# Carry copies on ScalarE, ten instead of eight states shared with GpSimd, an earlier front of the second chunk, and square-root tables loaded ahead

## The chip, the core and the metric

The kernel runs on one core of one Trainium2 chip. A core has five engines with a queue of instructions each: PE (TensorE, matrix products), DVE (VectorE), ACT (ScalarE), POOL (GpSimd) and SP (SyncE, which here issues most DMA transfers). The metric is the device time of one launch in microseconds. Before the change the median of three runs is 9530.28 us (9522.71 to 9545.77).

## The reference: what is computed

Four images of 256 channels and 64 x 64 points go through four layers, each of the form x = x + layer(group_norm(x)), one after the other:

- layer 0: a deformable 3 x 3 convolution, whose sampling points come from a convolution of the input,
- layer 1: attention over all 4096 points,
- layer 2: a second deformable convolution with 16 groups,
- layer 3: a selective state-space layer (Mamba), which reads the image as a sequence of 4096 points.

Each normalization needs sums over the whole image, so a layer can't begin its main work before the last point of the one before is there. Each ends with a square root and a reciprocal.

The change is mostly about layer 3. Cut to what matters there (512 inner channels d, 16 states n):

```
u, res = split(in_proj(x));  u = silu(causal_conv4(u) + conv_b)
dt, B, C = split(x_proj(u));  delta = softplus(dt_proj(dt) + dt_b)
for each point l:
    state[d, n] = exp(delta[d] * A[d, n]) * state[d, n] + delta[d] * u[d] * B[n]
    y[d] = sum_n state[d, n] * C[n]
out = out_proj((y + u * D) * silu(res))
```

## The kernel before

The images are worked on one after the other. `layer0`, `layer1`, `layer2` and `layer3` each get the image in SBUF as 2 x 128 channels by 4096 points (`x`).

**Layer 3** cuts the sequence into NC = 8 chunks of C = 512 points. In the scan loop a step s is one chunk j = s // 16 and one state n = s % 16, so there are 128 steps per image. The inner channels are four groups of 128 partitions (`dc` 0 to 3). A step does this:

- `product(s)` (line 1480, DVE): h = du * B[n] for all four groups, where du = delta * u. In a *helped* step DVE makes only three groups, and POOL makes the fourth into `hq` (`quarter`, line 1472), with a B row that SP fetches two steps ahead (`ahead`, tile `bs`). DVE's own B row `bn` is a matmul result in PSUM (`state`, line 1465).
- `scan(dc)`, four times: ACT makes da = exp(delta * A) into PSUM (line 1560), and DVE scans h along the chunk (line 1562). The pool for `da` has two buffers, so that the exponential of scan i waits for scan i - 2.
- the last column of the four scans is copied to `carry` for the same state of the next chunk (line 1582, POOL),
- POOL multiplies the whole h by C[n] (line 1585), in place,
- PE adds the four groups of h into the chunk's `y` in PSUM (line 1443), two steps later.

While chunk j - 1 is scanned, the *front* of chunk j (`front(j)`) makes its inputs: projections, causal convolution, Silu, then delta by way of Exp, two Identity operations and Ln on ACT (lines 1362 to 1378), three additions and the multiplication that makes `du` on POOL (lines 1371 to 1382). ACT splits the B rows into two bf16 parts (`split`, lines 1347 to 1355), POOL subtracting the first part in between. `close(j)` ends a chunk: `gated` on DVE (line 1531) and the output projection.

The order is written out by hand: the loop runs in `manual_schedule` for PE, ACT, DVE and POOL, and every engine works through its queue in the order of the program. `put(step, half, pe, rest)` gives the place of each piece of a front. Front j begins at loop step 16 (j - 1) - 5, and at 16 (j - 1) - 2 for j = 1, whose first steps are done by `first()` ahead of the loop. Half 0 is after the second scan of a step, half 1 after the fourth and ahead of the carry copy, half 2 after the multiplication by C. The single PSUM bank of the front (`bank()`) is handed from one piece to the next.

At the steps in `visits`, `product(s + 1)` is put in the middle of step s, between its second and third scan. These are the steps in which ACT does Silu and changes its function tables twice: step 5 of chunk 0 and step 2 of chunks 1 to 7.

**The normalizations.** `stats` collects means and variances on DVE, averages them over groups by two small matmuls, and takes the root on ACT (line 175, `rs`), which needs the table set with Sqrt. `scaled` and layer 3's opening wait for `rs`.

Of the kernel before, what the change touches and what calls it, by code (L numbers as in the profile page):

```python
# [9 lines left out]
F32 = mybir.dt.float32  # L10
I32 = mybir.dt.int32
BF16 = mybir.dt.bfloat16
AF = mybir.ActivationFunctionType
# [3 lines left out]
P = 128  # L17
# [6 lines left out]
NCH = N // 512  # L24
# [4 lines left out]
DS = 16  # L29
# [34 lines left out]
class Net:  # L64
# [346 lines left out]
    def layer1(self, x):  # L411
# [4 lines left out]
        with tc.tile_pool(name="l1a", bufs=1) as pa, tc.tile_pool(name="l1b", bufs=2) as pb:  # L416
# [167 lines left out]
            def divide(qb):  # L584
                b = blocks[qb]
                pd = wide("pden")[:, 0, :4]
                for t in range(4):
                    for i in range(2):
                        nc.tensor.matmul(  # L589
                            pd[:, t : t + 1],  # L590
                            b["acc"][:, bass.ds(512 * i + P * t, P)],
                            self.ones[:, 0:1],
                            start=(i == 0),
                            stop=(i == 1),
                        )
                b["rc"] = pb.tile([P, 4], F32, tag="rc", name="rc")
                nc.vector.reciprocal(b["rc"], pd)

            def spread(qb):

# [69 lines left out]
    def layer2(self, x):  # L670
# [5 lines left out]
        with (  # L676
# [196 lines left out]
            with tc.manual_schedule(  # L873
                engines={
                    mybir.EngineType.PE,
                    mybir.EngineType.Activation,
                    mybir.EngineType.DVE,
                    mybir.EngineType.Pool,
                }
            ):  # L880
                values(0)
                for t in range(T):
                    offsets(0, t)
                hats(0, 0)
# [12 lines left out]
                hats(1, 0)  # L897
                hats(1, 1)


                behind = None
                for p in range(last + 1):
                    near, far = p < last, p < last - 1
                    for wy in range(WIN):
                        product(p, wy, 0)
                        if near and wy == 0:
                            masked(p + 1)
                        product(p, wy, 1)
                        if wy == 1 and p > 1:
                            finish(p - 2)  # L910
                        if near and wy > 1:
                            gather(p + 1, wy - 2)
                        if near and wy < 3:
                            outer(p + 1, wy, nc.gpsimd)
                        prod = pairs(p)
                        if behind:
                            total(*behind)
                        behind = p, wy, prod
                        if wy == 0:
                            if near:  # L920
                                clear(p + 1)
                            if p:
                                nc.scalar.copy(made[p - 1]["o"].rearrange("p t c -> p (t c)"), made[p - 1]["pd"])
                        if far and wy < 2:
                            offsets(p + 2, wy)
                        if wy == 2:
                            if far:
                                hats(p + 2, 0)
                            if p < last:
                                values(p + 3)  # L930
                        if wy == 3:
                            if far:
                                hats(p + 2, 1)
                            if p:
                                turned(p - 1)
                        if wy == 4 and p:
                            project(p - 1)
                total(*behind)
                nc.scalar.copy(made[last]["o"].rearrange("p t c -> p (t c)"), made[last]["pd"])
                finish(last - 1)  # L940
                turned(last)
                project(last)
                finish(last)
# [137 lines left out]
    def layer3(self, x, out, nxt, early):  # L1081
# [10 lines left out]
        with (  # L1092
# [166 lines left out]
            def front(j):  # L1259
# [15 lines left out]
                put(0, 0, None, begin)  # L1275

                for dc in range(4):
                    at = ((0, 1), (1, 0), (1, 1), (4, 1))[dc]
                    put(*at, *project(j, dc, lambda dc=dc: c["up"][:, dc, 3:]))

                def convolve(dc):
# [58 lines left out]
                def split(i):  # L1340
# [21 lines left out]
                put(11, 0, None, lambda: nc.scalar.activation(c["du"], c["du"], AF.Exp, scale=-1.0))  # L1362
# [5 lines left out]
                put(12, 0, None, one)  # L1368


                put(11, 2, None, lambda: nc.gpsimd.tensor_add(c["delta"], c["delta"], c["du"]))
                put(
                    13,
                    1,
                    None,
                    lambda: nc.scalar.activation(c["du"], c["w"], AF.Identity, bias=self.ones[:, 0:1], scale=-1.0),
                )
                put(14, 1, None, lambda: nc.scalar.activation(c["w"], c["w"], AF.Ln))
# [3 lines left out]
                put(last, 2, None, lambda: nc.gpsimd.tensor_mul(c["du"], c["delta"], c["u"]))  # L1382
# [150 lines left out]
            with tc.manual_schedule(  # L1533
# [14 lines left out]
                for s in range(total):  # L1548
# [30 lines left out]
                    scan(2)  # L1579
                    scan(3)  # L1580
                    empty(s, 1)
                    nc.gpsimd.tensor_copy(carry[:, :, n : n + 1], h[:, :, C - 1 : C])  # L1582
                    cn = c.pop(("cn", n))
                    if s + 1 < total:
                        nc.gpsimd.tensor_mul(h, h, cn.to_broadcast([P, 4, C]))  # L1585
# [143 lines left out]
```

## Time and profile before

| | us |
|---|---|
| median of three runs | 9530.28 |
| profiled execution | 9708.01 |
| its span | 9706.1 |
| last image: layer 0, from `rs` to `rs` (7291.4 to 7837.9) | 546.5 |
| last image: layer 1 (to 8345.9) | 508.0 |
| last image: layer 2 (to 8734.1) | 388.2 |
| last image: layer 3 (to the end) | 972.0 |

| engine | busy us in the span | share |
|---|---|---|
| PE | 8526.4 | 88% |
| DVE | 7498.5 | 77% |
| POOL | 7032.0 | 72% |
| ACT | 4909.6 | 51% |

The table of stages is read from the ACT instruction that makes `rs`, which marks the start of each layer. The shares of busy time are averages over layers with different limits. In a row of the profile, `x` is the number of instructions, `|` is followed by the busy time in us and the mean of one in ns, and behind the next `|` stands the idle time of that engine just before these instructions, with what ended it. In rows in order of time the first two numbers are the start and the length in us.

### The profile page before, as it was taken

The page shows a single profiled execution, that of the slowest core. Times are in us where ns is not written, and L with a number is a line of the kernel's source. Part 1 is how long each engine was busy: PE and PEld are TensorE (multiplying, and loading weights), DVE is VectorE, ACT ScalarE, POOL GpSimd, SP SyncE. Part 2 cuts the span into 40 slices and gives each one's busy share as a digit, 9 for nine tenths or more (in the row PEclk, how much of TensorE's full clock was granted, in tenths as well). Part 3 has the DMA queues.
Part 4 walks back from the last instruction along what each step waited for, and adds up shares of the span by engine and source line. Part 5 has one row for each costly group of instructions (what it writes and reads, how often), then busy time and mean ns, then how long its engine had stood idle before and what let it go on. Part 6 is the DMA issues. An engine that isn't in the chain of part 4 may idle for free. (4 is left out here: it accounts for less than half of the span.)

```text
span 9706.1 us, 89200 instructions
## 1 busy us (share of the span) xinstructions
PE 8526.4 (88%) x29097; PEld 4207.1 (43%) x29097; DVE 7498.5 (77%) x8203; ACT 4909.6 (51%) x7568; POOL 7032.0 (72%) x4164
## 2 busy tenths in 40 slices
PE   4789998998778999899878899989987789998997
PEld 3643353443464344344346434434435643443443
DVE  4864498999676459899968645989996764588998
ACT  3743335665474333566557433366655743326664
POOL 3746686998574668699857467879984746777997
PEclk9999999999899999999989999999998999999999
DMA  7940011222793001122279201112218820111121
GB/s 262 328 151 1 26 49 52 67 66 69 266 329 126 1 30 47 56 66 67 66 288 329 102 1 35 47 57 66 66 63 312 324 82 1 38 52 51 62 62 52
DMA packets 414120, 1022.66 MB, mean 105 GB/s; under 512 B 38644, under 2 KB 111789, under 8 KB 411597
## 3 DMA queue, kind: packets, MB, share of 16 engines
q0 software_dynamic: 165888, 604.05, 17.2%
q1 hardware_dynamic: 247756, 412.80, 13.4%
q8 instruction: 233, 3.82, 0.2%
q14 instruction: 243, 1.98, 0.1%
HBM read 849.60 MB, written 93.37 MB: 97 GB/s over the span
## 5 line engine op out<-in xcount | busy, mean ns | idle before, releaser
L1585 POOL TENSOR_TENSOR h<-h,cn 128x2048 f32<-128x2048 f32 x508 | 2301.0, 4530 | 41.3 <-POOL carry L1582 0.6
L1562 DVE TENSOR_TENSOR_SCAN h<-da,carry,h 128x512 f32<-128x512 f32 x1800 | 2172.5, 1264 | 83.7 <-ACT da L1560 35.3
L1560 ACT ACTIVATE da<-delta,l3a 128x512 f32<-128x512 f32 x2048 | 1398.0, 690 | 1300.0 <-DVE h L1562 1297.0
L1443 PE MATMUL y<-h,ident 128*128 128x512 f32 x4096 | 1931.5, 607 | 11.7 <-POOL h L1585 11.7
L344 POOL DMA_INDIRECT g<-tab,idx x1152 | 1359.4, 1180 | 744.3 <-issue 427.8
L565 POOL TENSOR_TENSOR acc<-acc,e 128x1024 f32<-128x1024 f32 x480 | 1126.0, 2346 | 540.3 <-ACT e L561 519.0
L388 PE MATMUL pz<-cols,l0w 128*128 128x256 f32 x4608 | 1213.2, 410 | 188.7 <-issue 84.5
L1443 PEld LDWEIGHTS y<-h,ident 128*128 128x128 f32 x4096 | 797.1, 195 | 1188.0 <-issue 1070.9
L353 DVE SCALAR_TENSOR_TENSOR r<-g,wx,r 128x512 f32<-128x512 f32 x1152 | 858.3, 745 | 376.6 <-ACT r L352 246.9
L462 DVE TENSOR_REDUCE m<-pm 128x3 f32<-128x1536 f32 (+2 forms) x340 | 599.5, 1763 | 700.2 <-PE pm L452 700.2
L388 PEld LDWEIGHTS pz<-cols,l0w 128*128 128x128 f32 x4608 | 894.9, 205 | 358.0 <-DVE cols L377 111.4
L1480 DVE TENSOR_TENSOR h<-du,bn 128x2048 f32<-128x2048 f32 (+1 forms) x512 | 1025.0, 2002 | 26.7 <-POOL du L1382 24.8
L561 ACT ACTIVATE e<-sc 128x1024 f32<-128x1024 f32 x512 | 496.1, 1020 | 1029.6 <-PE sc L548 1029.5
L572 PE MATMUL cx<-e,v 128*128 128x512 f32 x2048 | 1000.6, 616 | 0.0
L845 DVE TENSOR_TENSOR prod<-ring,A 128x1280 f32<-128x1280 f32 x640 | 922.5, 1480 | 69.9 <-DMA ring<-ring 54.9
L352 ACT ACTIVATE r<-g,wx 128x512 f32<-128x512 f32 x1152 | 826.2, 717 | 258.4 <-DMA g<-tab,idx 210.9
L862 PE MATMUL pacc<-prod,ident 128*128 128x512 f32 x1920 | 913.4, 611 | 26.5 <-DVE prod L845 17.9
L854 POOL TENSOR_TENSOR prod<-prod 128x512 f32<-128x512 f32 x640 | 800.9, 1276 | 176.6 <-DVE prod L845 154.0
L370 PE MATMUL pt<-ident,acc 128*128 128x128 f32 x2304 | 427.3, 292 | 285.7 <-DVE acc L361 202.2
L572 PEld LDWEIGHTS cx<-e,v 128*128 128x128 f32 x2048 | 352.5, 189 | 599.5 <-issue 596.9
L360 ACT ACTIVATE acc<-r,wy 128x256 f32<-128x256 f32 x1152 | 571.3, 496 | 14.9 <-DVE r L353 9.8
L361 DVE SCALAR_TENSOR_TENSOR acc<-r,wy,acc 128x256 f32<-128x256 f32 x1152 | 549.1, 477 | 0.3
(256 smaller groups left out, 11027.6 us busy)
## 6 DMA issues: line engine op xcount, KB each, us to landing
cn<-cd SPq DMA_DIRECT2D x512, 256.0 KB
tab<-vt SPq DMA_DIRECT2D x112, 640.0 KB
bs<-cd SPq DMA_DIRECT2D x248, 256.0 KB
ring<-ring SPq DMA_DIRECT2D x288, 126.0 KB
ring<-ring SPq DMA_DIRECT2D x288, 124.0 KB
g<-tab,idx POOLq DMA_INDIRECT x1152
x<-in_x SPq DMA_DIRECT2D x64, 256.0 KB
out<-x SPq DMA_DIRECT2D x56, 256.0 KB
```

Source lines behind the costliest of these rows:

```text
L344: nc.gpsimd.indirect_dma_start(out=g[:], out_offset=None, in_=tab[:, :], in_offset=bass.IndirectOffsetOnAxis(ap=idx[:, t, k : k + 1], axis=0),
L353: nc.vector.scalar_tensor_tensor(r, g[:, :, 1, :], wx[:, 1, t, k : k + 1], r, ALU.mult, ALU.add)
L388: nc.tensor.matmul(sums[m][:, ot, :256], wf[:, i, bass.ts(ot, P)], cols[m][:, i, :], start=(i == 0), stop=(i == 17),)
L565: nc.gpsimd.tensor_add(b["acc"], b["acc"], e)
L572: nc.tensor.matmul(blocks[qb]["cx"], v[:, 4 * (i + kt // 4 * 4) + kt % 4, :], e[:, bass.ts(i % 2, 512)], start=(kt == 0 and i == 0), stop= ...
L845: nc.vector.tensor_mul(d["prod"][:, :, t, :].rearrange("p x (g c) -> p x g c", c=GC), ring[y // VR % 4][:, :, y % VR, :].rearrange("p x (g ...
L862: nc.tensor.matmul(d["pd"], self.ident, prod[:, wx, :], start=(wy == 0 and wx == 4), stop=(wy == WIN - 1 and wx == 2),)
L1443: nc.tensor.matmul(c["ys", dc], self.ident, h[:, dc, :], start=False, stop=(n == DS - 1))
L1480: nc.vector.tensor_mul(h[:, :d, :], c["du"][:, :d, :], c.pop(("bn", n)).to_broadcast([P, d, C]))
L1560: nc.scalar.activation(da, c["delta"][:, dc, :], AF.Exp, scale=al[:, dc, n : n + 1])
L1562: nc.vector.tensor_tensor_scan(h[:, dc, :], da, hb, carry[:, dc, n : n + 1], ALU.mult, ALU.add)
L1585: nc.gpsimd.tensor_mul(h, h, cn.to_broadcast([P, 4, C]))
```

## The change

1. The copy of the scans' last columns to `carry` goes from POOL to ACT.
2. A step is helped if its state is not 6 to 11, and it is not one of the last four of chunk 0: ten states per chunk (0 to 5 and 12 to 15) in place of eight (0 to 5, 14, 15). Chunk 0 keeps six.
3. The front of chunk 1 has other places: the fourth projection is later, the first three pieces of the convolution half a step to a step later, and Exp, Identity, Ln, the splits, the gates and POOL's four operations one to two steps earlier.
4. For chunks 2 to 7 the multiplication that makes `du` moves from step 18 half 2 to step 19 half 1 of the front, which is from behind the multiplication by C of state 13 to ahead of that of state 14. The other places are the same.
5. The table set with Sqrt is loaded ahead: in layer 1 by a square root of the last block's reciprocal (its result is not used), at the ends of layers 2 and 3 by a preload.

```diff
@@ layer1, divide
                 nc.vector.reciprocal(b["rc"], pd)
+                if qb == NCH - 1:
+                    root = self.small.tile([P, 1], F32, tag="root", name="root")
+                    nc.scalar.activation(root, b["rc"][:, 0:1], AF.Sqrt)
@@ layer2, the end
                 total(*behind)
+                nc.scalar.preload_act_table_set("sqrt_and_others")
                 nc.scalar.copy(made[last]["o"].rearrange("p t c -> p (t c)"), made[last]["pd"])
@@ layer3, front
                 for dc in range(4):
-                    at = ((0, 1), (1, 0), (1, 1), (4, 1))[dc]
+                    at = ((0, 1), (1, 0), (1, 1), (4, 1) if j > 1 else (5, 0))[dc]
                     put(*at, *project(j, dc, lambda dc=dc: c["up"][:, dc, 3:]))
...
                 for dc in range(4):
-                    at = ((2, 1) if j > 1 else (3, 0), (3, 1), (5, 1), (6, 1))[dc]
+                    at = (((2, 1), (3, 1), (5, 1), (6, 1)) if j > 1 else ((3, 1), (4, 1), (5, 1), (6, 1)))[dc]
                     put(*at, *convolve(dc))
...
+                at = dict(e=(11, 0), w=(12, 0), c=(13, 1), ln=(14, 1), s=((11, 0), (12, 1), (15, 0)), sums=(11, 14, 16, 19))
+                if j == 1:
+                    at = dict(e=(10, 1), w=(11, 1), c=(12, 1), ln=(13, 0), s=((11, 0), (12, 0), (13, 1)), sums=(10, 12, 13, 15))
                 for i in range(3):
-                    put((11, 12, 15)[i], i == 1, None, split(i))
+                    put(*at["s"][i], None, split(i))
...
-                put(11, 2, None, lambda: nc.gpsimd.tensor_add(c["delta"], c["delta"], c["du"]))
...
-                last = 18 if j > 1 else 16
-                put(14, 2, None, lambda: nc.gpsimd.tensor_add(c["delta"], c["delta"], c["du"]))
-                put((14 + last) // 2, 2, None, lambda: nc.gpsimd.tensor_add(c["delta"], c["delta"], c["w"]))
-                put(last, 2, None, lambda: nc.gpsimd.tensor_mul(c["du"], c["delta"], c["u"]))
...
+                for step, part in zip(at["sums"], ("du", "du", "w")):
+                    put(step, 2, None, lambda part=part: nc.gpsimd.tensor_add(c["delta"], c["delta"], c[part]))
+                put(at["sums"][3], 1 if j > 1 else 2, None, lambda: nc.gpsimd.tensor_mul(c["du"], c["delta"], c["u"]))

                 for dc in range(4):
-                    at = ((14, 0), (14, 1), (15, 0), (15, 1)) if j > 1 else ((11, 1), (12, 0), (12, 1), (13, 1))
+                    at = ((14, 0), (14, 1), (15, 0), (15, 1)) if j > 1 else ((11, 0), (11, 1), (12, 0), (12, 1))
                     put(*at[dc], *gate(j, dc))
@@ layer3, the helped steps
-            hs, helped = {}, [s for s in range(NC * DS) if s % DS in (14, 15, 0, 1, 2, 3, 4, 5) and s // 2 != 7]
+            hs, helped = {}, [s for s in range(NC * DS) if s % DS not in range(6, 12) and s // 4 != 3]
@@ layer3, the loop
-                    nc.gpsimd.tensor_copy(carry[:, :, n : n + 1], h[:, :, C - 1 : C])
+                    nc.scalar.copy(carry[:, :, n : n + 1], h[:, :, C - 1 : C])
...
+                nc.scalar.preload_act_table_set("sqrt_and_others")
                 for a in late:
```

In the changed kernel's queues the fourth projection of chunk 1 stands behind the first half of the y additions of step 2, and a layer-2 copy of the first ring comes ahead of the table load for layer 3's Exp.

More of the change, by code (lines that the diff above doesn't have):

```diff
@@ L1357, in split @@
                     return part
+                at = dict(e=(11, 0), w=(12, 0), c=(13, 1), ln=(14, 1), s=((11, 0), (12, 1), (15, 0)), sums=(11, 14, 16, 19))
+                if j == 1:
+                    at = dict(e=(10, 1), w=(11, 1), c=(12, 1), ln=(13, 0), s=((11, 0), (12, 0), (13, 1)), sums=(10, 12, 13, 15))
                 for i in range(3):
-                    put((11, 12, 15)[i], i == 1, None, split(i))
-                put(11, 0, None, lambda: nc.scalar.activation(c["du"], c["du"], AF.Exp, scale=-1.0))
+                    put(*at["s"][i], None, split(i))
+                put(*at["e"], None, lambda: nc.scalar.activation(c["du"], c["du"], AF.Exp, scale=-1.0))
                 def one():
@@ L1366, in one, with over @@
                     nc.scalar.activation(c["w"], c["du"], AF.Identity, bias=self.ones[:, 0:1])
-                put(12, 0, None, one)
-                put(11, 2, None, lambda: nc.gpsimd.tensor_add(c["delta"], c["delta"], c["du"]))
[L1372 to L1378, printed above, removed]
-                last = 18 if j > 1 else 16
-                put(14, 2, None, lambda: nc.gpsimd.tensor_add(c["delta"], c["delta"], c["du"]))
-                put((14 + last) // 2, 2, None, lambda: nc.gpsimd.tensor_add(c["delta"], c["delta"], c["w"]))
-                put(last, 2, None, lambda: nc.gpsimd.tensor_mul(c["du"], c["delta"], c["u"]))
+                put(*at["w"], None, one)
+                def over():
+                    nc.scalar.activation(c["du"], c["w"], AF.Identity, bias=self.ones[:, 0:1], scale=-1.0)
+                put(*at["c"], None, over)
+                put(*at["ln"], None, lambda: nc.scalar.activation(c["w"], c["w"], AF.Ln))
+                for step, part in zip(at["sums"], ("du", "du", "w")):
+                    put(step, 2, None, lambda part=part: nc.gpsimd.tensor_add(c["delta"], c["delta"], c[part]))
+                put(at["sums"][3], 1 if j > 1 else 2, None, lambda: nc.gpsimd.tensor_mul(c["du"], c["delta"], c["u"]))
                 for dc in range(4):
-                    at = ((14, 0), (14, 1), (15, 0), (15, 1)) if j > 1 else ((11, 1), (12, 0), (12, 1), (13, 1))
+                    at = ((14, 0), (14, 1), (15, 0), (15, 1)) if j > 1 else ((11, 0), (11, 1), (12, 0), (12, 1))
                     put(*at[dc], *gate(j, dc))
```

## The prediction

> **What bounds the kernel now.** The profiled execution took 9708.01 us around a span of 9706.1; the median of the runs is 9530.28, so 178 us belong to profiling. I work out differences in microseconds on the trace and take them from the median. The change reaches layer 3's scan loop and the starts of the normalizations, so I read the loop first, by stretches: the first chunk of the last image and a middle one (columns: length, then busy time and count of PE, its weight loads, DVE, ACT, POOL; clock; DMA share; GB/s).
>
> ```profile
> 8769.27:8895.26 125.99, 111.82 (x257) 47.51 (x257) 109.19 (x82) 77.03 (x109) 98.60 (x44) 0.97 0.15 45
> 9006.44:9117.61 111.17, 106.29 (x253) 45.99 (x252) 109.71 (x85) 73.94 (x102) 105.39 (x49) 1.00 0.20 63
> ```
>
> A middle chunk is DVE from end to end: 109.71 of 111.17. POOL (105.4) and PE (106.3) have about 5 us of room. The first chunk has 15 us that no engine fills. Then the groups by shape, for the durations:
>
> ```profile
> L1562 DVE TENSOR_TENSOR_SCAN h<-da,carry,h 128x512 f32<-128x512 f32 x1800 | 2172.5, 1264 | 83.7 <-ACT da L1560 35.3 <-DVE h L1480 3.2 <-ACT sres L1245 0.5
> L1480 DVE TENSOR_TENSOR h<-du,bn 128x2048 f32<-128x2048 f32 x264 | 596.5, 2259 | 0.0
> L1480 DVE TENSOR_TENSOR h<-du,bn 128x1536 f32<-128x1536 f32 x248 | 428.5, 1728 | 26.7 <-POOL du L1382 24.8 <-PE bn L1465 1.3
> L1472 POOL TENSOR_TENSOR hq<-du,bs 128x512 f32<-128x512 f32 x248 | 316.4, 1276 | 21.1 <-issue 20.8
> L469 ACT CAST t<-mx 128x4 bf16<-128x4 f32 x96 | 18.6, 193 | 87.6 <-DVE mx L472 76.6 <-DVE mx L465 11.0
> ```
>
> A step is one product and four scans. In time order a full step repeats every 7.09 us, a helped one every 6.56. DVE's own order shows where the first chunk waits (the bracket is the idle time before):
>
> ```profile
> 8812.29 1.28 DVE L1562 TENSOR_TENSOR_SCAN h<-da,carry,h 128x512 f32<-128x512 f32 x1 [2.23 <-ACT da L1560]
> ...
> 8862.36 2.46 DVE L1562 TENSOR_TENSOR_SCAN h<-da,carry,h 128x512 f32<-128x512 f32 x2 [3.43 <-ACT da L1560]
> ...
> 8895.26 1.75 DVE L1480 TENSOR_TENSOR h<-du,bn 128x1536 f32<-128x1536 f32 x1 [5.85 <-POOL du L1382]
> ```
>
> With the smaller ones (0.66, 0.42, 1.75, 0.15, 0.81) that is 15.3 us per image. ACT at steps 1 and 2 of a middle chunk:
>
> ```profile
> 9019.67 0.69 ACT L1560 ACTIVATE da<-delta,l3a 128x512 f32<-128x512 f32 x1 [0.47 <-DVE h L1562]
> 9020.38 1.28 ACT L1301 ACT_TABLE_LOAD   x1
> ...
> 9026.70 1.30 ACT L1560 ACTIVATE da<-delta,l3a 128x512 f32<-128x512 f32 x2
> ```
>
> and POOL from step 9 to the `du` product of step 13:
>
> ```profile
> 8965.12 0.19 POOL L1582 COPY carry<-h 128x4 f32<-128x4 f32 x1 [1.05 <-DVE h L1562]
> 8965.40 4.54 POOL L1585 TENSOR_TENSOR h<-h,cn 128x2048 f32<-128x2048 f32 x1
> ...
> 8999.27 4.53 POOL L1382 TENSOR_TENSOR du<-delta,u 128x2048 f32<-128x2048 f32 x1
> ```
>
> E(n) below is the moment at which DVE may start what follows step n's last scan.
>
> **Ten helped states.** In steps 12 and 13 of chunks 1 to 7 POOL makes the fourth quarter of the product. DVE saves 7.09 - 6.56 = 0.53 us, 14 times per image, on the bound. POOL pays 1.22 us each (its repetition in the trace), and SP issues one more 256 KB broadcast two steps ahead of use. By the Trainium skill (GPSIMD Engine Reference, Key points) GpSimd shares its SBUF interfaces with VectorE and contends with DVE instructions that have two SBUF inputs, which speaks against this. The trace shows such a case: `du<-delta,u` in the opening takes 1.42 us beside a POOL subtraction and 0.69 without one. If every added quarter cost DVE that 0.73, it would eat the gain: 0.73 against 0.53. But the loop's products read `bn` and its scans `da` from PSUM, and scans beside POOL keep their 1.26 us. I take no contention: -7.4 us per image.
>
> **The carry copy on ACT.** DVE had no part in it; POOL loses 0.27 us per step. What it adds is a wait. ACT works in order, and `da` has two buffers, so until now ACT made the next step's first `da` once scan 2 was done, 1.2 us before E, and the second at E. Now both stand behind the copy, which waits for scan 3. The copy's cost is unseen on ACT; the nearest row is the 128x4 cast at 0.193. From E: copy at 0.12, first `da` at 0.30, ready at 1.0; the second starts at 0.94 instead of 0.11, so everything behind it is 0.82 later. Usually the next product (1.83 or 2.36 to the first scan) hides that. Three places lack the cover:
> - Visits: eight steps per image make the next product early, so scan follows scan (1.18 apart). There scan 0 now waits for the full 1.0 us.
> - Step 2: Silu and two table loads, 6.4 us, stand between `da` 1 and `da` 2. `da` 2 ended at 9027.36, scan 2 began at 9027.61: 0.22 of slack, so 0.6 us lost. Queued behind them, nothing else is late. Chunks 1 to 6.
> - Step 6: two casts and an Exp, 3.1 us; `da` 2 was ready 0.2 before scan 2. Lost: 0.63, chunks 1 to 6.
>
> Its bounds: nothing, if DVE's release came early enough, to 1.3 per visit, were the copy as dear as the 0.26-us PSUM activations plus their handover.
>
> **`du` later.** For chunks 2 to 7 `du` moves from behind step 13's multiplication to step 14, behind `hq` 15, and `hq` 12 and 13 come before it. POOL, with the trace's repetition of 4.48 for a whole-tile and 1.22 for a quarter: from step 9's multiplication to `du`'s end were 8 x 4.48 + 4 x 0.275 (carries) + 0.2 + 1.22 = 38.36, as seen (8965.40 to 9003.76). Now 8 x 4.48 + 0.2 + 4 x 1.22 = 40.92. Step 9's multiplication also starts later: E(9) + 0.43 becomes E(9) + 0.95, since the copy stands behind Ln, which ends 0.68 after E(9). So `du` ends at E(9) + 41.9. DVE needs it at E(15) = E(9) + 2 x 7.09 + 4 x 6.56 = 40.4. The former margin of 2.7 becomes a stall of 1.5 us, 6 times per image, and `hq` 16, behind it, holds the last scan of the next step another 0.3. This is the term I am least sure of: 0 to 2.2.
>
> **A middle chunk**: -1.06 + 1.0 + 0.6 + 0.63 + 1.5 + 0.3 = +3.0. Six per image: +17.8. Chunk 7 has one visit (+1.0) and two savings (-1.06): nothing.
>
> **The first chunk.** Its front moves up: Exp to step 8, the split casts, Identity, Ln and gates one or two steps sooner, POOL's four `delta`/`du` operations to steps 8, 10, 11, 13. POOL's `du` then ends about 4 us before E(15): the 5.85 is gone. ACT's work is only moved. Laid end to end: step 9 has 1.8 us before `da` 2, late behind Exp: 0.7 lost; step 10 waits for POOL's subtraction before the second cast: 1.3; step 11 has Ln and two normalizations, 3.4 us: 1.7. Total 3.7 in place of 6.1. The fourth projection falls from step 2 to 3 in PE's queue, in front of convolution 2 there, which ends 1.4 us later; its ACT copy now stands before the carry copy: 1.7 at step 4, 0.9 for `bn` 5. Step 1's 0.66 goes. By step 6, its visit counted, 2.3 us are lost. Sum: +2.3 - 2.4 - 5.85 = -6.0 per image, bounded by -15 (all idle gone) and 0.
>
> **Square-root tables.** Eleven loads no longer stand in front of `rs`: those in layers 2 and 3 and in layer 0 of images 2 to 4 (layer 1's four stay).
>
> ```profile
> 8732.77 1.28 ACT L175 ACT_TABLE_LOAD   x1 [8.53 <-PE pv L173]
> 8734.06 0.26 ACT L175 ACTIVATE rs<-pv,eps 128x2 f32<-128x2 f32 x1
> ```
>
> The Trainium skill (ScalarE: Activation LUTs, What ACT_TABLE_LOAD costs) puts a switch at about 2.66 us, a drain included: 29 us for eleven. Here `rs` follows at 1.29, so 1.28 it is, and not always whole. Layer 0: 3 x 1.28. Layer 2's load began beside the statistics' matmul: 4 x 0.35. Layer 3's `rs` frees PE, but DVE waits for POOL's 12.4 us of `conv` and `diag` at 8741.2 anyway; PE's opening gains about 4 x 0.8. Sum -8.4. The new loads lie in ACT's idle 6 to 13 us before the last copies, hidden; without that cover each costs its 1.28. In layer 1 the table's activation waits for the last reciprocal, and behind it only the ring's zero copy is queued, which starts 5 us later anyway.
>
> **Sum**: 4 x (17.8 - 6.0) - 8.4 = +38.8 us: 9530 + 38 = 9568, profiled about 9744.
>
> **Rivals.**
> - `du` is not late: POOL's rows have some play, and DVE's new stalls would have to give it 1.5 us between steps 9 and 15. Against it, none of those stalls lies there. 38 - 24 x 1.8 = -5: 9525.
> - The copy's wait is free, so the change is faster. For it, ACT is busy half of the time; against it, the order of its queue and the 0.2 of slack. It takes away 24 x 2.2 at steps 2, 3 and 6, 8 x 1.0 at the other visits and 0.5 of each late `du`, 73 us: 9495. The sign turns where the copy costs less than half of what is reckoned here.
> - PE becomes the bound: step 13 to step 1 need 7.08 us each on PE (convolution 3.43, y 3.43, `bn` 0.2), more than a helped step's 6.56; if late multiplications hold it up, 1 to 2 us per chunk more: 9605.
>
> **Numbers.** Forecast 0.55, its own range 9550 to 9590; `du` in time 0.18; free copy 0.12; PE 0.15. 0.3% is 28.6 us, about what can be told from no change: the bounds are 9501.7 and 9558.9. Faster 0.12; same 0.18 plus the lower part of the forecast, 0.10; slower 0.60. The range leaves out most of the free copy and the top of PE: 9508 to 9608.
>
> **What shows it.** Right: scans after a visit idle 1.0 before ACT's `da`; a product idle 1.5 before POOL's `du` at the start of chunks 2 to 7, none at chunk 1; middle chunks near 114 us, the first near 120; no load before `rs` in layers 0 (but image 1's), 2 and 3. Wrong: middle chunks at or under 111, no `du` wait, or idle time before `bn` or y.

## The result and the profile after

| | us |
|---|---|
| changed kernel, median of 8 runs | 9568.92 (9552.19 to 9583.40) |
| kernel before, median of the 8 runs beside them | 9531.01 (9522.71 to 9545.77) |
| ratio | 1.0035, 95% interval 1.0024 to 1.0046 |
| profiled execution of the changed kernel | 9561.08, span 9559.3 |

The change makes the kernel 38 us slower, 23 to 44 by the interval. The forecast was 9568. That the two meet is partly luck: the terms of the sum, measured one by one, give about 25 us (below).

The lines that follow answer those of before. First the two stretches of the last image, the first chunk and a middle one, with the columns as before (length; busy time and count of PE, its weight loads, DVE, ACT, POOL; clock; DMA share; GB/s):

```profile
8613.16:8734.10 120.94, 109.05 (x247) 46.34 (x246) 109.36 (x81) 76.81 (x122) 95.82 (x30) 0.95 0.14 44
8847.75:8961.77 114.02, 107.45 (x253) 45.57 (x252) 109.16 (x84) 75.46 (x119) 104.87 (x35) 1.00 0.22 65
```

The first chunk fell from 125.99 to 120.94 us, the middle one rose from 111.17 to 114.02. DVE has less work there (109.16 us after 109.71) in a longer stretch: it waits 4.86 us instead of 1.46. The groups by shape, of the whole execution:

```profile
L1566 DVE TENSOR_TENSOR_SCAN h<-da,carry,h 128x512 f32<-128x512 f32 x1744 | 2111.0, 1265 | 120.5 <-ACT da L1564 73.2 <-DVE h L1484 1.4 <-ACT bt L1352 0.5
L1566 DVE TENSOR_TENSOR_SCAN h<-da,carry,hq 128x512 f32<-128x512 f32 x304 | 382.8, 1259 | 5.2 <-POOL hq L1476 5.2
L1484 DVE TENSOR_TENSOR h<-du,bn 128x1536 f32<-128x1536 f32 x304 | 525.8, 1730 | 36.8 <-POOL du L1386 33.3 <-PE bn L1469 3.5
L1586 ACT COPY carry<-h 128x4 f32<-128x4 f32 x512 | 100.7, 197 | 502.4 <-DVE h L1566 502.3
```

56 more products have three groups instead of four (x304 after x248), and one takes 1730 ns after 1728: a quarter on POOL costs DVE next to nothing in its other three. A scan takes 1265 ns after 1264. The waits for `da` grew from 35.3 to 73.2 us and those for `du` from 24.8 to 33.3. The new ACT copy takes 197 ns, by the nearest row 193.

DVE in order of time, in the last image: first waits of the first chunk, then, from 8847.75 on, a middle chunk: its start, its visit with the scan that follows it, its step 6 and its end:

```profile
8643.02 3.63 DVE L1566 TENSOR_TENSOR_SCAN h<-da,carry,h 128x512 f32<-128x512 f32 x3 [1.86 <-ACT da L1564]
8648.70 1.75 DVE L1484 TENSOR_TENSOR h<-du,bn 128x1536 f32<-128x1536 f32 x1 [0.88 <-PE bn L1469]
...
8665.56 2.26 DVE L1484 TENSOR_TENSOR h<-du,bn 128x2048 f32<-128x2048 f32 x1
...
8684.87 2.46 DVE L1566 TENSOR_TENSOR_SCAN h<-da,carry,h 128x512 f32<-128x512 f32 x2 [0.30 <-ACT da L1564]
8693.70 2.46 DVE L1566 TENSOR_TENSOR_SCAN h<-da,carry,h 128x512 f32<-128x512 f32 x2 [1.63 <-ACT da L1564]
8701.93 2.46 DVE L1566 TENSOR_TENSOR_SCAN h<-da,carry,h 128x512 f32<-128x512 f32 x2 [1.03 <-ACT da L1564]
8710.30 2.46 DVE L1566 TENSOR_TENSOR_SCAN h<-da,carry,h 128x512 f32<-128x512 f32 x2 [1.18 <-ACT da L1564]
...
8847.75 1.75 DVE L1484 TENSOR_TENSOR h<-du,bn 128x1536 f32<-128x1536 f32 x1 [1.34 <-POOL du L1386]
8849.61 3.63 DVE L1566 TENSOR_TENSOR_SCAN h<-da,carry,h 128x512 f32<-128x512 f32 x3
8853.47 1.28 DVE L1566 TENSOR_TENSOR_SCAN h<-da,carry,hq 128x512 f32<-128x512 f32 x1 [0.22 <-POOL hq L1476]
...
8869.80 1.28 DVE L1566 TENSOR_TENSOR_SCAN h<-da,carry,h 128x512 f32<-128x512 f32 x1 [0.45 <-ACT da L1564]
8871.00 1.26 DVE L1566 TENSOR_TENSOR_SCAN h<-da,carry,hq 128x512 f32<-128x512 f32 x1
8873.11 3.63 DVE L1566 TENSOR_TENSOR_SCAN h<-da,carry,h 128x512 f32<-128x512 f32 x3 [0.86 <-ACT da L1564]
...
8893.32 2.46 DVE L1566 TENSOR_TENSOR_SCAN h<-da,carry,h 128x512 f32<-128x512 f32 x2
8896.19 2.46 DVE L1566 TENSOR_TENSOR_SCAN h<-da,carry,h 128x512 f32<-128x512 f32 x2 [0.42 <-ACT da L1564]
...
8959.06 1.26 DVE L1566 TENSOR_TENSOR_SCAN h<-da,carry,hq 128x512 f32<-128x512 f32 x1
8961.77 1.75 DVE L1484 TENSOR_TENSOR h<-du,bn 128x1536 f32<-128x1536 f32 x1 [1.46 <-POOL du L1386]
```

Before, the same visit ran without a wait:

```profile
9028.80 1.25 DVE L1562 TENSOR_TENSOR_SCAN h<-da,carry,hq 128x512 f32<-128x512 f32 x1
9029.98 3.60 DVE L1562 TENSOR_TENSOR_SCAN h<-da,carry,h 128x512 f32<-128x512 f32 x3
```

At the first chunk's end there is no wait for `du` any more. In the middle chunk five new waits are seen: `du` at its start (and again at the start of the next chunk), `hq` 16, the third scan of step 2, the first scan after the visit, and the third scan of step 6. ACT beside them shows where those of step 2 and of the visit come from:

```profile
8861.34 0.20 ACT L1586 COPY carry<-h 128x4 f32<-128x4 f32 x1 [1.05 <-DVE h L1566]
8861.44 1.30 ACT L1564 ACTIVATE da<-delta,l3a 128x512 f32<-128x512 f32 x2
8862.76 1.28 ACT L1305 ACT_TABLE_LOAD   x1
...
8869.07 1.30 ACT L1564 ACTIVATE da<-delta,l3a 128x512 f32<-128x512 f32 x2
8872.29 0.20 ACT L1586 COPY carry<-h 128x4 f32<-128x4 f32 x1 [1.92 <-DVE h L1566]
8872.39 1.30 ACT L1564 ACTIVATE da<-delta,l3a 128x512 f32<-128x512 f32 x2
```

The scan that began at 8871.00 ends at 8872.26. The copy starts 0.03 later, `da` 0.10 after the start of the copy; `da` runs 0.69, and the scan begins at 8873.11. POOL, from step 9's multiplication to `du`:

```profile
8920.78 4.53 POOL L1589 TENSOR_TENSOR h<-h,cn 128x2048 f32<-128x2048 f32 x1 [2.40 <-ACT carry L1586]
...
8957.20 4.54 POOL L1386 TENSOR_TENSOR du<-delta,u 128x2048 f32<-128x2048 f32 x1
```

And the root that opens the last image's layer 3, with no table load ahead of it:

```profile
8576.32 0.26 ACT L175 ACTIVATE rs<-pv,eps 128x2 f32<-128x2 f32 x1 [8.54 <-PE pv L173]
```

**By layers.** The starts of `rs` cut the execution into layers (summed over the four images):

| | layer 0 | layer 1 | layer 2 | layer 3 |
|---|---|---|---|---|
| before | 2172.4 | 2031.6 | 1552.4 | 3879.0 |
| after | 2000.6 | 2030.9 | 1547.4 | 3909.5 |

Layer 0 differs by 172 us, of which the change touches only a table load. In it the gathers wait for nothing that the profile shows ("issue", 428 us of POOL before, 240 after). Over the twelve profiles of the experiments it lies anywhere from 2168 to 2242 us, while layer 1 stays within 2029 to 2033. So two profiles can only be compared in layers 1 to 3: there the change costs 7487.9 - 7462.9 = +25.0 us, inside the interval of the runs.

Cut further, layer 3 gives its sum by places (from `rs` to the first product, to the first `gated`, from `gated` to `gated` of the six chunks after it, of the last, and to the next `rs`). The first image:

| | opening | first chunk | six middle chunks | last chunk | end |
|---|---|---|---|---|---|
| before | 36.7 | 141.0 | 673.4 | 102.9 | 15.1 |
| after | 36.9 | 135.8 | 687.2 | 102.7 | 13.8 |

The middle chunks lose 13.8 us in each of the first three images and 15.8 in the last, 57.2 in all; the first chunks win 21.5.

### The profile page after: what moved, and what is told of

It reads as the page before. It is cut to its first block, busy times and chain, and to the rows that moved or that the text cites. A ratio compares the mean times of both kernels' runs of the same rounds, so it can differ in the third digit from the quotient of the medians.

```text
span 9559.3 us, 89643 instructions
## 1 busy us (share of the span) xinstructions
PE 8485.0 (89%) x29097; PEld 4153.3 (43%) x29097; DVE 7492.1 (78%) x8203; ACT 4965.7 (52%) x8085; POOL 6954.7 (73%) x3708
## 5 line engine op out<-in xcount | busy, mean ns | idle before, releaser
L1566 DVE TENSOR_TENSOR_SCAN h<-da,carry,h 128x512 f32<-128x512 f32 x1744 | 2111.0, 1265 | 120.5 <-ACT da L1564 73.2
L1447 PE MATMUL y<-h,ident 128*128 128x512 f32 x4096 | 1934.6, 607 | 39.0 <-POOL h L1589 38.8
L1564 ACT ACTIVATE da<-delta,l3a 128x512 f32<-128x512 f32 x2048 | 1366.4, 685 | 798.3 <-DVE h L1566 797.7
L344 POOL DMA_INDIRECT g<-tab,idx x1152 | 1321.5, 1147 | 607.3 <-issue 239.9
L388 PE MATMUL pz<-cols,l0w 128*128 128x256 f32 x4608 | 1155.2, 395 | 31.1 <-DVE cols L377 26.7
L1484 DVE TENSOR_TENSOR h<-du,bn 128x1536 f32<-128x1536 f32 (+1 forms) x512 | 996.0, 1945 | 36.9 <-POOL du L1386 33.3
L388 PEld LDWEIGHTS pz<-cols,l0w 128*128 128x128 f32 x4608 | 857.7, 196 | 180.3 <-DVE cols L377 80.1
```

The lines of the kernel that those rows point to most:

```text
L344: nc.gpsimd.indirect_dma_start(out=g[:], out_offset=None, in_=tab[:, :], in_offset=bass.IndirectOffsetOnAxis(ap=idx[:, t, k : k + 1], axis=0),
L388: nc.tensor.matmul(sums[m][:, ot, :256], wf[:, i, bass.ts(ot, P)], cols[m][:, i, :], start=(i == 0), stop=(i == 17),)
L1484: nc.vector.tensor_mul(h[:, :d, :], c["du"][:, :d, :], c.pop(("bn", n)).to_broadcast([P, d, C]))
L1564: nc.scalar.activation(da, c["delta"][:, dc, :], AF.Exp, scale=al[:, dc, n : n + 1])
L1566: nc.vector.tensor_tensor_scan(h[:, dc, :], da, hb, carry[:, dc, n : n + 1], ALU.mult, ALU.add)
```

## Experiments

The kernel before was timed beside each group of runs, at 9761, 9726 and 9759 us: layer 0 is slower there than in the first comparison. The ratios are taken within a group. The last column compares the traces in layers 1 to 3 with before's 7462.9 us.

| run | ratio (95% interval) | difference of medians, us | layers 1 to 3, us |
|---|---|---|---|
| the copy alone | 1.0063 (1.0049 to 1.0076) | +59.7 | +52.5 |
| ten states and `du` alone | 1.0034 (1.0023 to 1.0046) | +32.0 | +28.1 |
| the front alone | 0.9961 (0.9947 to 0.9975) | -35.2 | -32.0 |
| the tables alone | 0.9991 (0.9983 to 0.9999) | -7.9 | -8.4 |
| the whole again | 1.0034 (1.0020 to 1.0047) | +34.0 | +25.0 |
| the copy behind `da` | 1.0017 (1.0009 to 1.0024) | +15.2 | +13.0 |
| states 6 and 7 | 0.9973 (0.9965 to 0.9981) | -27.4 | -24.5 |
| both losing parts replaced | 0.9952 (0.9939 to 0.9965) | -44.5 | -36.3 |
| the whole, copy back on POOL | 0.9996 (0.9987 to 1.0005) | -8.6 | -12.5 |
| the whole, eight states | 1.0015 (1.0008 to 1.0022) | +11.7 | +14.2 |
| front, tables, states 6 and 7 | 0.9945 (0.9932 to 0.9958) | -58.5 | -67.1 |
| the same with eleven states | 0.9933 (0.9921 to 0.9945) | -71.6 | -70.4 |

The two ways of measuring agree within 10 us in every row.

### The four parts, each alone

The copy:

```diff
-                    nc.gpsimd.tensor_copy(carry[:, :, n : n + 1], h[:, :, C - 1 : C])
+                    nc.scalar.copy(carry[:, :, n : n + 1], h[:, :, C - 1 : C])
```

> The kernel before with one line changed: the carry's last columns are copied by ScalarE. Queue-wait theory: the next step's first da stands behind the copy. With the waits that the changed kernel's trace shows (0.86 us at each of 8 visits per image, 0.41 at step 6 of chunks 1 to 6, about 0.5 at step 2 of them where nothing else stands in VectorE's queue) and no help for the first chunk's GpSimd chain, the four images pay 27 + 10 + 4 us = about +41, less up to 8 that GpSimd's shorter chain gives back in the first chunk: 9564 to 9572 us, and the scans idle before ScalarE's da by some 40 us more than before. Rival (the wait is free, and the loss of the whole change lies in the late du and the helped quarters): 9522 to 9531 us.

Measured: +60 us, more than the queue-wait theory had, and the rival of a free wait is out. DVE in this kernel's order of time, at the end of the first chunk, at a visit and at step 6:

```profile
4127.09 1.75 DVE L1480 TENSOR_TENSOR h<-du,bn 128x1536 f32<-128x1536 f32 x1 [7.40 <-POOL du L1382]
...
4265.98 3.63 DVE L1562 TENSOR_TENSOR_SCAN h<-da,carry,h 128x512 f32<-128x512 f32 x3 [0.86 <-ACT da L1560]
...
4289.05 2.46 DVE L1562 TENSOR_TENSOR_SCAN h<-da,carry,h 128x512 f32<-128x512 f32 x2 [0.41 <-ACT da L1560]
```

The last two waits are those of the changed kernel. What the expectation missed: in the first chunks the copy gives nothing back but takes another 9.2 us in all (1.9 to 3.1 per image), the wait for `du` among it (7.40 after 6.57 in the same image). And a bracket is less than a wait costs: scans that follow one another start 1.18 us apart though one takes 1.26, so they overlap by 0.08, and a wait takes the overlap too. The scan ahead of the visit began at 4263.86: 2.12 apart, 0.94 more than 1.18.

Ten states with `du` behind `hq` 15:

```diff
-            hs, helped = {}, [s for s in range(NC * DS) if s % DS in (14, 15, 0, 1, 2, 3, 4, 5) and s // 2 != 7]
+            hs, helped = {}, [s for s in range(NC * DS) if s % DS not in range(6, 12) and s // 4 != 3]
...
-                put(last, 2, None, lambda: nc.gpsimd.tensor_mul(c["du"], c["delta"], c["u"]))
+                put(*((19, 1) if j > 1 else (last, 2)), None, lambda: nc.gpsimd.tensor_mul(c["du"], c["delta"], c["u"]))
```

> The kernel before with GpSimd making the fourth quarter of B's product in steps 12 and 13 too (ten states), and du behind hq 15; the copy stays on GpSimd. Lateness theory: the two quarters (1.22 us each) and four copies (0.27) put du 2 us behind VectorE's need, so chunks 2 to 7 each wait 2.0 us for du and 0.5 for hq 16, and save 2 x 0.53: +1.5 us six times per image, less 1.06 in chunk 7: about +32 us, 9563. Rival (GpSimd keeps up, the helped quarters are worth their 0.53 each): 56 x 0.53 = -30 us, 9501. A second rival (the quarter costs VectorE as much as it saves, by contention): no stall before du, steps 12 and 13 still at 7.09, 9531.

Measured: +32 us, with the waits at the expected places and of the expected size:

```profile
4219.15 1.75 DVE L1480 TENSOR_TENSOR h<-du,bn 128x1536 f32<-128x1536 f32 x1 [1.97 <-POOL du L1382]
4225.11 1.28 DVE L1562 TENSOR_TENSOR_SCAN h<-da,carry,hq 128x512 f32<-128x512 f32 x1 [0.47 <-POOL hq L1472]
```

A middle chunk takes 113.94 us after 112.35 (+1.6), the last, which has no successor to make a `du` for, 101.8 after 102.86: the saving is there, 1.04 us for two quarters, and is lost wherever POOL has a `du` to make. Two edits act together here: `du` now also waits behind `hq` 15, a third quarter of 1.22 us that used to come after it. No run moved `du` alone, so the shares in its 1.97 us are not told apart.

The front alone has the diff's places for j == 1 (the fourth projection, the convolutions, splits, Exp, gates and POOL's four operations) and none of the rest:

> The kernel before with the first chunk's front alone moved up (its fourth projection, convolutions, casts, Exp, gates and GpSimd's four operations). Theory: the 5.85 us wait for du at the end of the first chunk goes, and about 1.3 of new waits for ScalarE come, so some -5 to -7 us per image as the changed kernel's first chunk shows (121.0 against 126.0 us): -20 to -28 us, 9503 to 9511. Rival (the waits only move to ScalarE within the chunk): 9527 to 9531.

Measured: -35 us, by the trace 6.2 to 7.4 per first chunk: the theory's direction, and the upper end of its size or more, since without the copy ahead of it ACT keeps DVE waiting less (0.21, 0.51 and 0.93 us at steps 9 to 11, where the changed kernel has 0.30, 1.63 and 1.03). Against that, the scan that opens step 4 waits 2.98 us in this kernel and 1.86 in the changed one. Why was not asked. With the tables and states 6 and 7 beside it (below) the same front takes 132.05 us for the first chunk of the first image instead of 133.56.

The tables alone:

```diff
+                if qb == NCH - 1:
+                    root = self.small.tile([P, 1], F32, tag="root", name="root")
+                    nc.scalar.activation(root, b["rc"][:, 0:1], AF.Sqrt)
...
+                nc.scalar.preload_act_table_set("sqrt_and_others")
...
+                nc.scalar.preload_act_table_set("sqrt_and_others")
```

> The kernel before with the root's table loaded early, nothing else. Theory: eleven loads of 1.28 us leave the way, four of them nearly hidden already and four that open layer 3 worth 0.8 each: -8.4 us, 9522. Rival by the dearer price of a switch (2.66 us each): -29 us, 9502. Rival (what follows rs waits for something else anyway): 0, 9531.

Measured: -7.9 us by the runs (the interval allows 1 to 17), -8.4 by layers 1 to 3. The dearer price is out. So is zero: the ends of layer 3 in the first three images, where three loads of 1.28 went, are 1.0 to 1.6 us shorter.

### The whole again, and with one part undone

> The changed kernel once more, beside the other runs. The four parts alone came to 1.0063 (the copy), 1.0034 (ten states), 0.9961 (the front) and 0.9991 (the tables). If they add up, the whole is 1.0049. By the trace of layer 3 alone (before 3878.9 us; copy +50.1, ten states +27.8, front -31.8, whole +30.6) the parts overlap: the copy takes 16 x 0.27 us off GpSimd's chunk, so that du is 1.45 us late in the whole and not 2.05 as beside GpSimd's copy; that gives +31 and -8 of tables, 1.0024 to 1.0035.

The change unaltered, beside the other kernels: 1.0034. The parts overlap as expected: `du` comes 1.46 late in the whole and 1.97 in the ten states alone.

With the copy back on POOL (the one line of the first experiment, reversed):

> The changed kernel with one line undone: the last columns are copied by GpSimd again. If the parts add in layer 3 (ten states +27.8 us over four images, front -31.8, tables -2.1 there and -4 in layer 2), du is 1.95 us late at each of six chunk starts instead of 1.45, and the visits wait for nothing: -10 us, 0.999 of before, and 45 us faster than the changed kernel. Rival (without the copy on ScalarE GpSimd is so late that what the copy's waits give back is lost again): as the changed kernel, 1.003.

Measured: 0.9996, 39 us of layer 3 less than the whole (3870.7 after 3909.5). So the copy costs 39 us in the whole and 50 alone; the difference is what it spares POOL's chain (with the copy on POOL `du` is 1.95 us late and `hq` 16 0.47, with it on ACT 1.45 and 0.22).

With eight states, and `du` where it was:

> The changed kernel without its third part: eight helped states and du where they were before; the copy on ScalarE, the front and the tables stay. Added up in layer 3: copy +50.1, front -31.8, tables -2.1, and -4 in layer 2: +12 us, 1.0013 of before, 20 us faster than the changed kernel, with no wait for du at chunks 2 to 7. Rival (the copy makes the room that the two quarters need, so that they pay beside it): slower than the changed kernel, 1.004 or more.

Measured: 1.0015; the ten states cost 11 us of layer 3 in the whole (3898.5 before them, 3909.5 with them). There is no wait for `du` at chunks 2 to 7.

### Is it the queue's order?

The copy stays on ScalarE, but is put behind the next step's first two `da`, and POOL's multiplication, which overwrites the columns, behind it:

```diff
+                    def leave(s=s, h=h, n=n, cn=cn):
+                        nc.scalar.copy(carry[:, :, n : n + 1], h[:, :, C - 1 : C])
+                        nc.gpsimd.tensor_mul(h, h, cn.to_broadcast([P, 4, C]))
+                        empty(s, 2)
...
                     scan(0)
                     scan(1)
+                    if leaving:
+                        leaving.pop()()
                     quarter(s + 1)
```

> The kernel before with ScalarE's copy of the last columns as in the changed kernel, but queued behind the next step's first two da instead of ahead of them; GpSimd's multiplication, which overwrites the columns, follows the copy and starts some 0.7 us later. Queue-order theory: the waits of 0.86 us at visits and 0.41 at step 6 go, since no da stands behind a copy that waits for scan 3; the time goes from before's +0.6% (the copy ahead of da) to within 0.15% of before. Rival (ScalarE's copy costs by being there, by its reading h or by its handover, or GpSimd's later multiplication is felt): +0.4 to +0.7% again.

Measured: +0.17%, a quarter of the plain copy's 0.63 and just above what was expected. DVE in this kernel, at the first chunk's end, at an `hq` 15 and at a visit:

```profile
4093.22 1.75 DVE L1480 TENSOR_TENSOR h<-du,bn 128x1536 f32<-128x1536 f32 x1 [8.63 <-POOL du L1382]
...
4204.04 1.28 DVE L1562 TENSOR_TENSOR_SCAN h<-da,carry,hq 128x512 f32<-128x512 f32 x1 [0.37 <-POOL hq L1472]
...
4228.78 1.25 DVE L1562 TENSOR_TENSOR_SCAN h<-da,carry,hq 128x512 f32<-128x512 f32 x1
4229.96 3.60 DVE L1562 TENSOR_TENSOR_SCAN h<-da,carry,h 128x512 f32<-128x512 f32 x3
```

And ACT at that visit:

```profile
4228.90 0.69 ACT L1560 ACTIVATE da<-delta,l3a 128x512 f32<-128x512 f32 x1 [1.98 <-DVE h L1562]
4230.07 0.69 ACT L1560 ACTIVATE da<-delta,l3a 128x512 f32<-128x512 f32 x1 [0.48 <-DVE h L1562]
4230.70 0.18 ACT L1587 COPY carry<-h 128x4 f32<-128x4 f32 x1
```

The scans at the visit stand 1.18 apart again, and step 6 has no wait. The same copy costs nothing at a visit when `da` is ahead of it. The six middle chunks of four images cost 8.6 us together, beside the plain copy 39.8. What is left are waits for POOL, which starts its multiplications later: `du` of the first chunk is waited for 8.63 us (6.57 before in this image), and `hq` 15 0.37 in each middle chunk. The first chunks lose 9.4 us, as much as beside the plain copy.

### Is it the quarters, or where they stand?

Two more helped states again, but 6 and 7 instead of 12 and 13, with `du` at its old place:

```diff
-            hs, helped = {}, [s for s in range(NC * DS) if s % DS in (14, 15, 0, 1, 2, 3, 4, 5) and s // 2 != 7]
+            hs, helped = {}, [s for s in range(NC * DS) if s % DS in (14, 15, 0, 1, 2, 3, 4, 5) and s // 2 != 7 or s % DS in (6, 7) and s > DS]
```

> The kernel before with two more helped states per chunk as in the ten-state run, but states 6 and 7 in place of 12 and 13, and du left where it was; GpSimd idles 1.07 us ahead of step 5's copy and 1.10 ahead of step 6's, where the two quarters (1.22 us each) fall. Theory (a helped quarter is worth its 0.53 us wherever GpSimd has room, and the loss with 12 and 13 is only du's lateness): -1.06 in seven chunks of four images, -30 us, less up to 12 if hq 15, now some 0.8 us later, is waited for: -0.2 to -0.3%. Rival (two more quarters cost VectorE what they save, by contention or by the broadcast's transfers): within 0.05% of before, or the +0.34% of the ten-state run.

Measured: -0.27%, 59 us better than two quarters at 12 and 13 with `du` moved. The products keep their length (1728 ns, x304). `hq` 15 is not waited for. A middle chunk falls by 0.70 instead of 1.06, for another reason:

```profile
4117.80 1.28 DVE L1562 TENSOR_TENSOR_SCAN h<-da,carry,h 128x512 f32<-128x512 f32 x1 [0.26 <-ACT da L1560]
```

That is step 6, in which ACT has two casts and an Exp between `da` 1 and `da` 2; a product shortened by 0.53 uncovers them.

### Better versions

Both losing parts replaced (front and tables as in the change, the copy behind `da`, states 6 and 7):

> The change with its two losing parts mended: front and tables as they are, the copy on ScalarE behind the next step's two da, states 6 and 7 helped in place of 12 and 13, du where it was before. If the parts add: -35 (front) - 8 (tables) - 30 (two states) and about 0 for the copy: -70 us, 0.993 of before. If the deferred copy costs what the plain one does: 0.998.

Measured: 0.9952, -36 us in layers 1 to 3. The expectation took the copy as nothing; with the 13 us that it costs alone the sum of the four rows is -32.0 - 8.4 - 24.5 + 13.0 = -52, still 16 more than came. Eight or nine of these are in layer 3 (-41 by its rows, -32 seen), but not in the first chunk, where the parts add: 135.4 us, against 133.6 of the front alone and 1.8 to 2.9 for the deferred copy. Cut by places, 6.6 are in the last chunks, and most of that is scatter counted several times: with unchanged code the last chunk takes 1.7 us more or less in single images (before: 102.86, 104.55 and 102.86 in the first three), and before's 104.55 is in each of the four rows. The other seven are in layers 1 and 2; layer 1 alone scatters by 4 us from profile to profile.

With the copy left on POOL:

> What gained alone, together: the front, the tables, and two more helped states per chunk at states 6 and 7; the copy on GpSimd, du where it was before. Added up in layer 3: -31.8 - 22.6 - 2.1, and -4 in layer 2: -60 us, 0.9938 of before. Rival (front and quarters want the same room on GpSimd): -45 us or less, 0.9953.

Measured: 0.9945. Layers 1 to 3 give -67.1; the parts alone sum to -64.9. They don't compete for POOL: there is no wait for `du`. The match of the sums is partly luck, since the first chunks gain 8 us more than the parts alone (mostly the 1.5 per image seen at the front) and the other places less.

And with an eleventh state, the copy on ScalarE in states 8 to 13 alone:

```diff
+                    columns = nc.scalar.copy if s > DS and 8 <= n <= 13 else nc.gpsimd.tensor_copy
+                    columns(carry[:, :, n : n + 1], h[:, :, C - 1 : C])
```

> The kernel of the run before it and three edits for chunks 2 on: state 13 is helped too, the copy goes to ScalarE in states 8 to 13 alone (no visit lies there, and a full product of 2.26 us covers the wait), du behind hq 15. Theory: GpSimd gives up 6 x 0.27 us and takes 1.22, so du stays in time and each chunk saves another 0.53 us: -15 us beside the run before it, 0.9923 of before. Rival (the copies wait on ScalarE behind Exp, Identity and Ln, and GpSimd's chain of du grows by these waits): a wait before du of 1 us or more, no gain or a loss of up to 10 us beside it.

Measured: 0.9933, the best of all, but not told from the run before it (the intervals meet; layer 3 is 3816.2 after 3817.2 us). `du` is in time, as the theory had it, but `hq` 16 behind it isn't:

```profile
4187.38 1.28 DVE L1565 TENSOR_TENSOR_SCAN h<-da,carry,hq 128x512 f32<-128x512 f32 x1 [0.39 <-POOL hq L1475]
```

0.39 and the lost overlap of 0.08 are nearly the 0.53 that the eleventh quarter saves: a middle chunk takes 111.65 us after 111.68.

## Why the prediction was right, and where it wasn't

**A middle chunk.** Each term, with its measured size in the last image. A wait is measured here from start to start against the same pair without it, so that the lost overlap counts:

| term | predicted | measured | from |
|---|---|---|---|
| two more quarters | -1.06 | -1.04 | last chunk of the ten states alone |
| after the visit | 1.0 | 0.93 | 8871.00 to 8873.11, less 1.18 |
| step 6 | 0.63 | 0.51 | 8893.32 to 8896.19, 2.87 instead of 2.36 |
| step 2 | 0.6 | about 0.5 | bracket 0.45, last image and chunk 1 |
| `du` | 1.5 | 1.54 | 8959.06 to 8961.77, less 1.17 |
| `hq` 16 | 0.3 | 0.31 | 8849.61 to 8853.47, less 3.55 |
| sum | 3.0 | 2.75 | stretches: 114.02 - 111.17 = 2.85 |

**`du`**, the term called least sure, was the best. From E(9) (8919.83, where the next product starts) POOL's multiplication begins at +0.95, as worked out; from there to `du`'s end are 40.96 us, worked out as 40.92; DVE wants it at E(9) + 40.4 (8959.06 and the usual 1.17), as worked out. Adding up one engine's queue from the trace's own repetitions was enough.

**The copy.** The mechanism held, and the deferred copy shows it. The working put the copy at E + 0.12 and `da` at E + 0.30; with E at 8872.18, which is 1.18 after 8871.00, they start at E + 0.11 and E + 0.21. The copy takes 0.10 us of ACT's time instead of 0.18. The rest of the wait is `da` itself, 0.69, which used to run beside scan 3, and the two handovers. So the free-copy rival was worded wrongly: a copy of no length would still cost most of this. What decides is which instruction stands ahead of which.

**Step 2 in images 1 to 3** is the step of the sum that failed by size. The 0.6 was read in the last image, and taken for all four. In the first three images DVE has statistics of the next image to make in chunks 2 to 7 (`BATCH_NORM_STATS2`, between the visit's product and the third scan of step 2), and these hide the wait. In the second image before the change:

```profile
4211.94 1.72 DVE L1480 TENSOR_TENSOR h<-du,bn 128x1536 f32<-128x1536 f32 x1
4213.58 1.28 DVE L152 BATCH_NORM_STATS2 st<-x 128x6 f32<-128x512 f32 x2
4214.78 1.26 DVE L1562 TENSOR_TENSOR_SCAN h<-da,carry,h 128x512 f32<-128x512 f32 x1
```

In the changed kernel the wait of 0.45 stands in chunk 1 of these images and in none of their chunks 2 to 6. These rise by 2.3, not 3.0. Fifteen chunks without the 0.6 are 9 of the 14 us by which the middle chunks were put too dear: altogether they cost 57 us, predicted 71. Most of the rest is the smaller sizes in the table.

**The first chunk.** -5.1 to -5.7 per image, predicted -6.0. The "15 us that no engine fills" are DVE's idle time alone: through most of the 5.85 POOL was making `du` (8890.72 to 8895.22). That wait went, as said. The product of step 7 divides the chunk:

```profile
8819.37 2.26 DVE L1480 TENSOR_TENSOR h<-du,bn 128x2048 f32<-128x2048 f32 x1
```

From the first product to this one were 50.10 us before, 52.40 after (to 8665.56): +2.30, predicted +2.3. Behind it the chunk gained 7.35, predicted 8.25. Of the waits for ACT, step 4's were put at 1.7 (measured 1.86), `bn` 0.9 (0.88), step 9 0.7 (0.30), step 10 1.3 (1.63), step 11 1.7 (1.03); step 12's 1.18 was not foreseen. The late waits sum to 4.14 against 3.7, right as a sum rather than one by one.

**The tables**: -8.4 predicted, -8.4 measured in layers 1 to 3 and -7.9 by the runs. The total meets better than its parts: the starts of layer 0 gained 3.8 (predicted 3.84), those of layer 3 2.0 (3.2: layer 2 is 3.6 shorter, and the openings take 1.7 of it back), those of layer 2 2.5 (1.4; layer 1, in which this shows, scatters by 4). The rest comes out near zero. The trace's 1.28 per load was the price, and for loads beside other work less. The 2.66 of the Trainium skill (ScalarE: Activation LUTs, What ACT_TABLE_LOAD costs), a drain included, would have made 29: no run shows a drain at these loads.

**Contention.** The rule of the Trainium skill that was weighed (GPSIMD Engine Reference, Key points) names two SBUF inputs, and it does not bite here. In the changed kernel a three-group product takes 1.730 us beside POOL's multiplication by C (236 of the 304), 1.729 beside a quarter (32; most quarters run beside scans) and 1.726 beside neither (32). A scan takes 1.260 us beside a quarter and 1.263 beside neither. That fits the reading that one of their inputs lies in PSUM; no run varied that alone.

**The sum.** Predicted +38.8; measured in layers 1 to 3 +25, by the runs +38 and +34 (intervals from 19 to 46). The middle chunks were 14 us too dear, which is most of the difference from +25. What the runs have beyond the traced layers would lie in layer 0, and its scatter hides it.

**The profiled time** was wrong: 9744 was forecast by carrying over before's 178 us between profile and median, and it came to 9561. That excess was not profiling (9561.08 is one of the changed kernel's eight timed runs, profiled) but layer 0, 172 us slower in that execution.

**The rivals.** `du` in time: no, 1.46 late. Free copy: no, +60 alone. PE as the bound: no; a middle chunk stays within the forecast of DVE's waits, which are for ACT and POOL, and the only waits for `bn` are in the first chunk.

## What to carry to other kernels

Moving a small instruction to a half-idle engine is priced by what stands behind it in that engine's queue: list the next instruction there, who waits for it and with how much cover, and put the small one behind it if its own consumer can wait. Work given to a helper engine is worth its saving only where that engine has idle time ahead of its next deadline; two quarters gained 27 us at states 6 and 7 and lost 32 at 12 and 13, where `du` had to come behind them. Read a wait's cost from start to start, and look for cover in every repetition, not in the last one only.

## What was not expected of the hardware

- A 128x4 copy on ScalarE has a row of 0.20 us, but the next activation starts 0.10 after the copy's start, and the copy starts 0.03 after the scan that it waits for ends (8872.26 to 8872.29 to 8872.39).
- Back to back, DVE's scans overlap by 0.08 us (1.18 apart, 1.26 long), which a wait in between takes away on top of its bracket.
- The layer with the gathers took from 2001 to 2242 us in different executions, while attention behind it stayed within 2029 to 2033. It is the likely source of before's 9531 and 9761 us in different groups of runs: 9531 less its layers 1 to 3 and the 71 us ahead of the first `rs` leaves 1997 us for layer 0. No profile of the kernel before at that level was taken, and what makes the gathers slower stays open. The four single parts ran on one chip and the other experiments on a second, which gave both 9726 and 9759; the first comparison's chip is not on record, so a difference between chips is not ruled out.
